# Sums of gathered tiles tied to an even beat, and the first group's ranks with 128 columns of weights, in a graph layer on one core

## The chip, the core and the metric

The kernel runs on one core of a Trainium2 chip. The metric is the device time of the program in microseconds (us), without the profiler: the median of the runs. The engines are TensorE (PE in the profile, PEld for its weight loads), VectorE (DVE), ScalarE (ACT), GpSimd (POOL) and SyncE (SP), each with an instruction queue of its own that is worked off in order. SP and POOL issue most DMAs here.

## The reference

A graph layer with 6,250 nodes of 128 features and 100,000 edges, sorted by target node. Each edge carries a message, the source's row times one of two weight matrices (by the type of the edge). Messages are summed at the target, a third matrix's product is added, then ReLU, the residual and a normalisation over the features.

```python
Xs = X[src]
m_data = Xs @ W_data.T + b_data
m_ctrl = Xs @ W_control.T + b_control
msg = jnp.where((edge_types == 0)[:, None], m_data, m_ctrl)
agg = jax.ops.segment_sum(msg, dst, num_segments=X.shape[0])
out = jax.nn.relu(agg + (X @ W_self.T + b_self))
return _layernorm(X + out, axis=-1)
```

## The kernel before

**Build.** The nodes are 49 blocks of 128 rows. For each block the kernel multiplies the rows with the two message matrices (`y`, L465 and L467) and splits the f32 result into three bf16 parts that add up to it (`yh`, `y1`, `ym`, `y2`, `yl`: copies on ACT or DVE, matmuls with `minus` at L483 and L496). The three parts stay in SBUF as `m3` (98 tables of 128 rows by 3 × 128) and are also stored to DRAM as `table`, part by part, in seven pairs of stores on SP (L509). Parts hold 4, 8, 8, 8, 8, 8 and 5 blocks; they are numbered from 0.

**Two ways to sum.** Target blocks 0 to 34 are in seven groups of five and are summed from SBUF ("windowed" blocks). Blocks 35 to 48 are summed from DRAM ("gathered" blocks): for each, 18 tiles of 128 edges are fetched by POOL with an indirect DMA from `table` (`msg`, L877), and TensorE adds each one into the block's sum with a one-hot matrix as weights (`gm`, tile `agg_g`, L231). There are 14 × 18 = 252 such tiles. `msg` has MB = 5 buffers: a fetch can start when the fifth sum before it is done. DVE makes the one-hot matrices for six tiles at once (`gh`, tile `hot_g`).

**Windowed blocks.** For each group the edges that fall into its window are sorted into buckets by source table. `fields` and `hot` prepare one-hot matrices (`hot_st`), and a rank of each edge within its bucket is found in 18 steps: TensorE adds `tri` times the one-hot matrix into an accumulator (`tri`, tile `acc`), DVE reads the ranks out (`rank`, tile `slot`, L584), TensorE adds the remainder (`rest`). Both matmuls go through the helper `by_columns` (L231), which makes four matmuls with 32 columns of weights each of one with 128. Once six steps are ranked, DVE makes `two` and TensorE writes the edges' numbers into their slots (`v`, tile `small`, L621, ten matmuls for a step). After the 18th, ACT copies the slots (`vs`), SP stores them (`packed`, L639) and loads them back as a broadcast to all partitions (`rows`, L739), one load for a block. DVE turns that into one-hot weights (`sel`, L746); TensorE gathers from `m3` with them (`g`, tile `g_ps`, L775), ACT copies the result out (`e`, tile `gs`, L790), and TensorE sums it into the target rows (`s`, tile `agg`, L231). A block takes 25 tiles of `g` and as many of `s`. Then come `o` (the product with the third matrix), `whole`, `sum`, and normalisation and store, a group at a time (`root`, `scale`, `apply`, `out`).

**Order.** Nothing in the order of the instructions is left to the chip. Each kind of step is a generator that names the step, what it costs on which engine, and what it needs. `Order.run` plays them through on a clock of its own and always takes the step that can start first; among those that can start within 0.1 us of each other the one with the earliest due time (`due`). `BUILT`, `BLOCK` and `PACE` set the due times. So a changed cost or due time moves instructions of all engines, whether or not the chip's times agree with the planner's. In it a step `msg` keeps POOL busy for `PACE` and is there 3.0 us after its start.

Of the kernel before, what the change touches and what calls it, by code (L numbers as in the profile page):

```python
# [19 lines left out]
P = 128  # L20
# [7 lines left out]
KT = 18  # L28
# [24 lines left out]
CH = 6  # L53
KC = 6
# [4 lines left out]
class Order:  # L59
# [10 lines left out]
    CLOSE = 0.1  # L70

    def __init__(self):
        self.free = dict.fromkeys("TVAGS", 0.0)
        self.end = {}

    def run(self, streams, due):
# [24 lines left out]
def step(name, costs, *needs, lag=0.0):  # L101
    return as_tuple(name), costs, [as_tuple(n) for n in needs], lag
# [111 lines left out]
def sums_over_windows(ctx, tc, x, xt, edges, w, bias, table, packed, total,  # L214
                      add_parts, finish, load_rows, norm):
    nc = tc.nc
    V, A, G, T = nc.vector, nc.scalar, nc.gpsimd, nc.tensor
# [7 lines left out]
    order = Order()  # L225
    YB = 4

    def by_columns(out, lhsT, rhs, **flags):

        for c in range(0, P, 32):  # L230
            T.matmul(out[c : c + 32], lhsT[:, c : c + 32], rhs, **flags)  # L231


    r0 = const.tile([EC, RJ], I32, name="r0")
# [49 lines left out]
    for j in range(RJ):  # L284
# [7 lines left out]
        out=er.rearrange("p k c -> p (k c)"), out_offset=None,  # L292
# [90 lines left out]

    LEAD, BUILT = 6.0, 76
    BLOCK = 13.1
    PACE = 1.68
    AHEAD, FIRST = 26.0, 20

    def due(kind, *i):
# [35 lines left out]
        if kind in ("rows", "sel", "d", "g", "e", "s"):  # L425
            of = {"rows": 1, "sel": 1, "d": 2}.get(kind, NS)
            lead = {"rows": -9, "sel": -3, "d": -1, "g": 0, "e": 1, "s": 2}[kind]
            return BUILT + BLOCK * (i[0] + (i[1] / of if len(i) > 1 else 0)) + lead
        if kind in ("gh", "gm", "msg"):
            k = i[1] * CH if kind == "gh" else i[1]  # L430
            return BUILT + PACE * (i[0] * KT + k) + {"msg": 0, "gh": 2, "gm": 5}[kind]
        n = GROUPS[i[0]]
        end = BUILT + BLOCK * STARTS[i[0]] - (AHEAD if i[0] else FIRST)
        span = BLOCK * n if i[0] else 34.0
# [136 lines left out]
    def ranks():  # L571
        for grp, n in enumerate(GROUPS):
            free = [("rank", grp - 1, KT - 1)] if grp else []
            for k in range(KT):
                yield step(("tri", grp, k), {"T": 0.21}, ("hot", grp, k // KC), *free)
                if k == 0:
                    acc = ps_a.tile([P, 512], F32, name="acc")
                    flat = acc[:, : n * NT]
                    by_q = flat.rearrange("p (s q) -> p q s", q=n)
                hot = hots[grp, k // KC][:, k % KC].rearrange("p s q -> p (s q)")  # L580
                by_columns(flat, tri, hot, start=k == 0, stop=False, skip_group_check=True)
                free = []
                yield step(("rank", grp, k), {"V": 0.13 + 0.103 * n}, ("tri", grp, k))
                V.tensor_reduce(slots[grp][:, k, :], by_q, axis=AX.X, op=ALU.max)  # L584
                if k == KT - 1:
                    break
                yield step(("rest", grp, k), {"T": 0.21}, ("rank", grp, k))
                by_columns(flat, rest, hot, start=False, stop=k == KT - 2, skip_group_check=True)

    def fill_a():  # L590
        for grp, n in enumerate(GROUPS):
# [16 lines left out]
    def fill_b():  # L608
        for grp, n in enumerate(GROUPS):
            free = [("listed", grp - 1)] if grp else ["first"]  # L610
            for k in range(KT):
                yield step(("v", grp, k), {"T": 0.07 * n}, ("two", grp, k // KC), *free)
                if k == 0:
                    vts[grp] = ps_a.tile([P, 512], F32, name="small")
                vt = vts[grp][:, : (n + 1) // 2 * NT].rearrange("p (j s) -> p j s", s=NT)
                two = two_s[grp, k // KC]
                hot = hots[grp, k // KC]
                for q in range(n):
                    for i in range(2):
                        c0 = (q % 2 * 2 + i) * R  # L620
                        T.matmul(vt[c0 : c0 + R, q // 2, :], two[:, k % KC, i, :, q],  # L621
                                 hot[:, k % KC, :, q], start=k == 0 and q < 2,
                                 stop=k == KT - 1, skip_group_check=True)
                free = []
# [247 lines left out]
    def gather_rows():  # L872
        for i, (j, k) in enumerate(gathered):
            free = [("gm", *gathered[i - MB])] if i >= MB else [*stored, "idx"]
            yield step(("msg", j, k), {"G": PACE}, *free, lag=3.0 - PACE)
            msgs[j, k] = late.tile([P, D3], BF16, name="msg", bufs=MB)
            G.indirect_dma_start(  # L877
                out=msgs[j, k], out_offset=None, in_=table[:, :],
                in_offset=bass.IndirectOffsetOnAxis(ap=idx[:, j, k : k + 1], axis=0),
            )  # L880

    def gathered_hots():
        chunks = [(j, c) for j in range(NG) for c in range(KT // CH)]
# [9 lines left out]
    def gathered_sums():  # L893
        for j, k in gathered:
            free = [("agg", NPB + j)] if k == 0 else [("o", NPB + j)] if k == KT - 1 else []
            yield step(("gm", j, k), {"T": 0.165}, ("msg", j, k), ("gh", j, k // CH), *free)
            if k == 0:
                aggs[NPB + j] = ps_a.tile([P, D3], F32, name="agg_g")
            by_columns(aggs[NPB + j], g_hots[j, k // CH][:, :, k % CH], msgs.pop((j, k)),
# [28 lines left out]
    def close_build():  # L928
# [9 lines left out]
        normalise([(lambda g=g: (hs_[g], mvs[g]), STARTS[g] + q0, q0, n) for g, q0, n in PIECES], "p"), add_up(), gather(), evict(), to_hots(), bucket_hots(),  # L938
        multiply(), take(0, "yh", "y"), leave(0, "y1", "yh"),
        take(1, "ym", "y1"), last_part(), constants(), store(), close_build(), add_counts(),  # L940
        finish_gathered(), gathered_sums(), gathered_hots(), gather_rows(), gathered_fields(),
        normalise([(lambda i=i: kept[i], NPB + i * GQ, 0, min(GQ, NG - i * GQ))
                   for i in range(-(-NG // GQ))], "g"),
        load_own("p", list(range(NPB)), XS),
# [128 lines left out]
```

## Time and profile before

| what | value |
|---|---|
| median of 3 runs without the profiler | 627.68 us (622.87 to 630.16) |
| the profiled execution's own time | 542.67 us |
| its span, first to last instruction | 540.9 us |
| mean granted TensorE clock in it | 0.984 |
| busy: PE, DVE, ACT, POOL | 507.3, 432.4, 415.9, 297.4 us |
| matmuls | 11,204 |

Durations below are from the one profiled execution. Busy time is a union of recorded intervals on an engine, and matmuls overlap in it. "Idle before" names what ended an engine's idle time. The chain of work follows the last instruction back, at each step to what released it. A granted clock of 0.5 in a window means that TensorE ran at half speed there.

### The profile page before, as it was taken

The numbers are of one execution on the slowest core, as the hardware profiler recorded it, in microseconds if no ns is written. First come the engines' busy times: TensorE is split into PE (matmuls) and PEld (weight loads), VectorE is DVE, ScalarE is ACT, GpSimd is POOL, SyncE is SP. The second block draws the span as 40 slices with busy tenths as digits, with TensorE's granted clock in tenths as the row PEclk, the third lists the DMA queues.
The fourth block names the chain that finished last, engine by engine and source line by source line (L and its number), as shares of the span: only waits on it lengthen the run. The fifth ranks groups of instructions, "written<-read, shape, count | busy, mean of one in ns | idle before, by whom it ended". The sixth has DMA issues, their size and how long they took to land.

```text
span 540.9 us, 26355 instructions
## 1 busy us (share of the span) xinstructions
PE 507.3 (94%) x11204; PEld 442.9 (82%) x11204; DVE 432.4 (80%) x967; ACT 415.9 (77%) x1003; POOL 297.4 (55%) x267
## 2 busy tenths in 40 slices
PE   5799977999999999999999999999999999999993
PEld 3546547799887998988989899999998999889882
DVE  5587889578987789978799878999789667668784
ACT  6654356577869788798888888877979879889793
POOL 1000002777687676776567676775757756677500
PEclk9999998799999999999999999999999999999998
DMA  3566875542555425554354542544445454555301
GB/s 94 145 179 191 260 239 193 153 131 79 184 159 161 138 77 179 157 169 134 99 194 139 164 139 81 183 139 160 142 134 162 133 156 135 180 166 164 115 17 35
DMA packets 60932, 79.19 MB, mean 146 GB/s; under 512 B 15760, under 2 KB 51371, under 8 KB 60807
## 3 DMA queue, kind: packets, MB, share of 16 engines
q1 hardware_dynamic: 47253, 49.14, 27.8%
q0 software_dynamic: 12400, 25.08, 16.9%
q10 hardware_dynamic: 1154, 3.21, 1.9%
q8 instruction: 89, 1.46, 1.1%
q14 instruction: 36, 0.29, 0.2%
HBM read 64.35 MB, written 13.05 MB: 143 GB/s over the span
## 4 chain that ended last, share of the span: by engine, by line
PE 73%; DMA 9%; ACT 5%; DVE 5%; issue 3%; SPq 3%; POOL 1%; ACTq 0%; DVEq 0%; POOLq 0%
PE agg L231 25%; PE g_ps L775 23%; PE acc L231 8%; PE agg_g L231 7%; PE small L621 6%; DMA msg<-table,idx 5%; ACT gs L790 2%; DMA rows<-packed 2%; PE y L465 2%; SPq L807 1%; POOL msg L877 1%; ACT h_p L189 1%; SPq L158 1%; DVE slot L584 1%; DVE hot_st L567 1%
## 5 line engine op out<-in xcount | busy, mean ns | idle before, releaser
L790 ACT CAST gs<-g_ps 128x384 bf16<-128x384 f32 x807 | 333.7, 498 | 72.4 <-PE g_ps L775 53.5
L877 POOL DMA_INDIRECT msg<-table,idx x252 | 288.5, 1145 | 115.4 <-PE g_ps L775 46.4
L775 PE MATMUL g_ps<-m,rows 128*32 128x384 bf16 x3430 | 322.4, 332 | 0.9 <-ACT gs L790 0.7
L231 PE MATMUL agg<-gs,hot_d 128*32 128x384 bf16 x3360 | 301.4, 331 | 3.3 <-ACT gs L790 3.3
L231 PEld LDWEIGHTS <-hot_d 128*32 128x32 bf16 x3500 | 195.8, 137 | 13.1 <-issue 7.1
L775 PEld LDWEIGHTS <-rows 128*32 128x32 bf16 x3430 | 189.8, 137 | 18.5 <-issue 12.7
L231 PE MATMUL agg_g<-msg,hot_g 128*32 128x384 bf16 x1008 | 109.1, 332 | 6.2 <-DMA msg<-table,idx 5.8
L584 DVE TENSOR_REDUCE slot<-acc 128x5 bf16<-128x490 f32 x126 | 83.6, 663 | 28.9 <-PE acc L231 17.7
L760 DVE TENSOR_TENSOR hot_d<-count,to 128x1664 bf16<-128x1664 bf16 x70 | 74.4, 1065 | 6.6 <-PE agg L231 6.0
L621 PE MATMUL small<-hot_st,two 128*32 128x98 bf16 x1260 | 70.2, 290 | 0.0
L231 PE MATMUL acc<-hot_st,tri 128*32 128x490 bf16 x504 | 61.8, 376 | 2.1 <-DVE hot_st L567 2.1
L231 PEld LDWEIGHTS <-hot_g 128*32 128x32 bf16 x1008 | 53.5, 123 | 10.6 <-issue 7.8
L231 PE MATMUL acc<-hot_st,rest 128*32 128x490 bf16 x476 | 56.8, 378 | 4.5 <-DVE slot L584 4.0
L621 PEld LDWEIGHTS <-two 128*32 128x32 bf16 x1260 | 58.3, 118 | 2.3 <-DVE two L605 0.6
L715 POOL DMA_INDIRECT mixed<-table,row_i x7 | 6.5, 933 | 92.9 <-DVE hot_g L889 82.3
L476 ACT CAST m<-y 128x512 bf16<-128x512 f32 (+1 forms) x50 | 28.1, 577 | 30.9 <-PE y L483 23.1
L567 DVE TENSOR_TENSOR hot_st<-count,st_b 128x2940 bf16<-128x2940 bf16 x21 | 41.8, 1996 | 7.6 <-PE small L621 5.3
L746 DVE TENSOR_SCALAR rows<-rows,pid 128x3136 bf16<-128x3136 bf16 x35 | 37.0, 1057 | 5.5 <-DMA rows<-packed 5.2
L153 DVE TENSOR_REDUCE whole<-agg 128x128 f32<-128x384 f32 x35 | 19.4, 553 | 17.6 <-PE agg L231 12.8
L465 PE MATMUL y<-w_sb,xt 128*128 128x256 f32 x98 | 33.2, 426 | 0.0
L231 PEld LDWEIGHTS <-rest 128*32 128x32 bf16 x476 | 22.1, 98 | 12.8 <-issue 11.8
L231 PEld LDWEIGHTS <-tri 128*32 128x32 bf16 x504 | 22.4, 99 | 3.3 <-issue 3.1
(144 smaller groups left out, 438.0 us busy)
## 6 DMA issues: line engine op xcount, KB each, us to landing
rows<-packed SPq DMA_DIRECT2D x35, 784.0 KB
table<-m SPq DMA_DIRECT2D x10, 768.0 KB
msg<-table,idx POOLq DMA_INDIRECT x252
xt<-in_xt ACTq DMA_DIRECT2D x5, 512.0 KB
xt_p<-in_xt SPq DMA_DIRECT2D x35, 64.0 KB
xs_p<-in_x SPq DMA_DIRECT2D x35, 64.0 KB
out<-h_p SPq DMA_DIRECT2D x6, 320.0 KB
table<-m SPq DMA_DIRECT2D x2, 480.0 KB
```

The lines of the kernel that those rows point to most:

```text
L153: nc.vector.tensor_reduce(whole, agg.rearrange("p (i c) -> p c i", i=3), axis=AX.X, op=ALU.add)
L231: T.matmul(out[c : c + 32], lhsT[:, c : c + 32], rhs, **flags)
L465: T.matmul(y[:, j, :], xts[g][:, b + j - at_part[g], :], w_sb[:, : 2 * D], start=j == 0, stop=False, skip_group_check=True)
L476: A.copy(part_of(b, n, i), ys[b][:, :n, :].rearrange("p b (t c) -> p t b c", t=2))
L567: V.tensor_tensor(hot, counted[n][:, None, 1 : NT + 1, :].to_broadcast([P, KC, NT, n]), fields[grp][2][:, c * KC : c * KC + KC, None, :].t ...
L584: V.tensor_reduce(slots[grp][:, k, :], by_q, axis=AX.X, op=ALU.max)
L621: T.matmul(vt[c0 : c0 + R, q // 2, :], two[:, k % KC, i, :, q], hot[:, k % KC, :, q], start=k == 0 and q < 2, stop=k == KT - 1, skip_group ...
L746: V.tensor_scalar(rows[b], rows[b], pid1, None, op0=ALU.is_equal)
L760: V.tensor_tensor(hot, counted[DC][:, :, :n], places[grp][:, q, None, c * DC : c * DC + n].to_broadcast([P, P, n]), op=ALU.is_equal)
L775: T.matmul(g_ps[t * R : (t + 1) * R, :D3], rows[b][:, :, s], m3[:, s, :], start=True, stop=True)
L790: (A.copy if e == "A" else V.tensor_copy)(gs[at], g_tiles.pop((b, g))[at, :D3])
L877: G.indirect_dma_start(out=msgs[j, k], out_offset=None, in_=table[:, :], in_offset=bass.IndirectOffsetOnAxis(ap=idx[:, j, k : k + 1], axis=0),
```

## The change

Three things change. The ranks of group 0 are made with weights of 128 columns (`width`), one matmul where there were four; the other groups keep 32. The slots of group 0 are written in chunks: all 60 matmuls of six steps in one planner's step. And the sums of gathered tiles get a beat: a fictitious engine "C" in the planner, on which a step `beat` of `PACE` runs for every gathered tile from 4 us after the table's stores are planned to be in; `gm` waits for its beat and gets an earlier due time. `msg` now costs POOL 1.25 in the planner and its data is there 3.0 us after that; `PACE` is 1.75 instead of 1.68. The beat puts no instruction on the chip: it only moves the planned place of `gm`.

```diff
@@ class Order
-        self.free = dict.fromkeys("TVAGS", 0.0)
+        self.free = dict.fromkeys("TVAGSC", 0.0)
...
-    def by_columns(out, lhsT, rhs, **flags):
-
-        for c in range(0, P, 32):
-            T.matmul(out[c : c + 32], lhsT[:, c : c + 32], rhs, **flags)
+    def by_columns(out, lhsT, rhs, width=32, **flags):
+
+        for c in range(0, P, width):
+            T.matmul(out[c : c + width], lhsT[:, c : c + width], rhs, **flags)
...
-    PACE = 1.68
+    PACE = 1.75
...
+        if kind in ("beat", "beating"):
+            return 0.0
         if kind in ("gh", "gm", "msg"):
             k = i[1] * CH if kind == "gh" else i[1]
-            return BUILT + PACE * (i[0] * KT + k) + {"msg": 0, "gh": 2, "gm": 5}[kind]
+            return BUILT + PACE * (i[0] * KT + k) + {"msg": 0, "gh": 2, "gm": 0}[kind]
...
@@ def ranks():
+            width = 32 if grp else P
...
-                by_columns(flat, tri, hot, start=k == 0, stop=False, skip_group_check=True)
+                by_columns(flat, tri, hot, width, start=k == 0, stop=False, skip_group_check=True)
...
-                by_columns(flat, rest, hot, start=False, stop=k == KT - 2, skip_group_check=True)
+                by_columns(flat, rest, hot, width, start=False, stop=k == KT - 2, skip_group_check=True)
...
@@ def fill_b():
-                yield step(("v", grp, k), {"T": 0.07 * n}, ("two", grp, k // KC), *free)
+                if grp:
+                    yield step(("v", grp, k), {"T": 0.07 * n}, ("two", grp, k // KC), *free)
+                elif k % KC == 0:
+                    yield step(("v", grp, k + KC - 1), {"T": 0.07 * n * KC}, ("two", grp, k // KC), *free)
...
@@ def gather_rows():
-            yield step(("msg", j, k), {"G": PACE}, *free, lag=3.0 - PACE)
+            yield step(("msg", j, k), {"G": 1.25}, *free, lag=3.0)
...
+    def beats():
+
+        yield step("beating", {"C": 4.0}, *stored, "idx")
+        for i, (j, k) in enumerate(gathered):
+            yield step(("beat", j, k), {"C": PACE}, "beating")
...
@@ def gathered_sums():
-            yield step(("gm", j, k), {"T": 0.165}, ("msg", j, k), ("gh", j, k // CH), *free)
+            yield step(("gm", j, k), {"T": 0.165}, ("msg", j, k), ("beat", j, k), ("gh", j, k // CH), *free)
```

The first place where the order moves is SP's queue, at the end of the build. Before, the slots of group 0 stand behind the loads of block 3, and the stores of table part 5 come after the first three `rows`:

```order
L807 DMA xt_p_958<-in_xt 128x128
L158 DMA xs_p_960<-in_x 128x128
L639 DMA packed_61<-vs0_151 32x3x98
L639 DMA packed_61<-vs0_151 32x2x98
L739 DMA rows_1124<-packed_61 128x3136
L739 DMA rows_1126<-packed_61 128x3136
L739 DMA rows_1141<-packed_61 128x3136
L509 DMA table_60<-m3_157 128x8x384 x2
L509 DMA table_60<-m3_157 128x5x384 x2
```

Now the pair of part 5 (eight blocks) stands ahead of `packed`:

```order
L813 DMA xt_p_844<-in_xt 128x128
L158 DMA xs_p_846<-in_x 128x128
L511 DMA table_60<-m3_157 128x8x384 x2
L645 DMA packed_61<-vs0_151 32x3x98
L645 DMA packed_61<-vs0_151 32x2x98
L745 DMA rows_1030<-packed_61 128x3136
L745 DMA rows_1034<-packed_61 128x3136
L745 DMA rows_1036<-packed_61 128x3136
L511 DMA table_60<-m3_157 128x5x384 x2
```

The loads ahead of it are the same as before in number, so `packed` has two more stores in front of it, of 768 KB each.

The second place is TensorE's queue in the build, between the seventh and the eighth step of group 0's ranks. Before, four weight loads and matmuls with 32 columns for `rest` and as many for `tri` (the three repeats of each are left out) stand between matmuls with 128 columns:

```order
L467 MATMUL y<-bias_104,ones_b 128x256
L231 LDWEIGHTS rest
L231 MATMUL acc<-hot_st,rest 32x490
...
L231 LDWEIGHTS tri
L231 MATMUL acc<-hot_st,tri 32x490
...
L621 LDWEIGHTS two
L621 MATMUL small<-hot_st,two 32x98
```

Now it is one each; the 60 matmuls of `v` follow, with 32 columns as before:

```order
L469 MATMUL y<-bias_104,ones_b 128x256
L231 LDWEIGHTS rest
L231 MATMUL acc<-hot_st,rest 128x490
L231 LDWEIGHTS tri
L231 MATMUL acc<-hot_st,tri 128x490
L627 LDWEIGHTS two
L627 MATMUL small<-hot_st,two 32x98
```

The number of changes between matmuls of 128 and of 32 columns falls from 46 to 15, counted from the first rank matmul to the first of `g_ps`.

The third place is TensorE's queue at the seventh and eighth gathered tile of block 35. Before, their sums follow each other directly (buffer numbers are kept; of four equal pairs of rows one is shown):

```order
L621 MATMUL small_1267<-hot_st_865,two_1794 32x98
L231 LDWEIGHTS hot_g_1933
L231 MATMUL agg_g_1591<-msg_1785,hot_g_1933 32x384
...
L231 MATMUL agg_g_1591<-msg_1845,hot_g_1933 32x384
L231 LDWEIGHTS tri_143
L231 MATMUL acc_950<-hot_st_1066,tri_143 32x490
```

Now six tiles of windowed blocks, a step of `v` and a `rest` stand between them (most are left out):

```order
L231 MATMUL agg_g_1421<-msg_1490,hot_g_1664 32x384
L231 LDWEIGHTS hot_d_1348
L231 MATMUL agg_1685<-gs_1718,hot_d_1348 32x384
...
L781 LDWEIGHTS rows_1034
L781 MATMUL g_ps_1795<-m3_157,rows_1034 32x384
...
L231 LDWEIGHTS rest_144
L231 MATMUL acc_867<-hot_st_966,rest_144 32x490
L231 LDWEIGHTS hot_g_1664
L231 MATMUL agg_g_1421<-msg_1545,hot_g_1664 32x384
```

Counted over the whole queue in tiles of `g` and `s`: ahead of the first gathered sum stand 42 before and 32 now; behind the last one 86 before and 23 now. The smallest number over five spacings is 16 before and 19 now.

More of the change, by code (lines that the diff above doesn't have):

```diff
@@ L940, in sums_over_windows @@
         take(1, "ym", "y1"), last_part(), constants(), store(), close_build(), add_counts(),
-        finish_gathered(), gathered_sums(), gathered_hots(), gather_rows(), gathered_fields(),
+        finish_gathered(), gathered_sums(), gathered_hots(), gather_rows(), gathered_fields(), beats(),
         normalise([(lambda i=i: kept[i], NPB + i * GQ, 0, min(GQ, NG - i * GQ))
```

## The prediction

> **What bounds the kernel now.** I read the page's busy shares first, then the windows of equal length, then the chain of work and the waits of TensorE.
>
> ```profile
> PE 507.3 (94%) x11204; PEld 442.9 (82%) x11204; DVE 432.4 (80%) x967; ACT 415.9 (77%) x1003; POOL 297.4 (55%) x267
> PE 73%; DMA 9%; ACT 5%; DVE 5%; issue 3%; SPq 3%; POOL 1%; ACTq 0%; DVEq 0%; POOLq 0%
> ```
>
> TensorE is busy for 94% of the span and carries 73% of the chain that ended last. A busy record is longer than the time a matmul takes from its successor:
>
> ```profile
> 240.37 0.40 PE L231 MATMUL agg<-gs,hot_d 128*32 128x384 bf16 x4
> 240.53 0.40 PE L775 MATMUL g_ps<-m,rows 128*32 128x384 bf16 x4
> ```
>
> A tile (four matmuls beside each other, one for each 32 columns of weights) is recorded as 0.40 us, but the next one starts 0.16 us later. So 0.16 us is the price of a tile, and a wait shorter than about 0.24 us leaves no idle time in a record. Where TensorE does idle in the long stage is in the waits from 95 to 520 us (engine, what it waited for: total, times, longest):
>
> ```profile
> PE agg_g L231 <- DMA msg<-table,idx: 5.8, 7, 3.5
> PE agg L231 <- ACT gs L790: 3.3, 6, 1.0
> PE acc L231 <- DVE slot L584: 0.8, 3, 0.3
> ```
>
> The largest item is the one that the change is about: a sum over a gathered tile (`gm`) waiting for its message. Since hidden stalls count too, I went through the starts in the timeline:
>
> ```profile
> 104.23 0.39 PE L231 MATMUL agg<-gs,hot_d 128*32 128x384 bf16 x4
> 104.89 0.38 PE L231 MATMUL agg_g<-msg,hot_g 128*32 128x384 bf16 x4 [0.27 <-DMA msg<-table,idx]
> 514.45 0.39 PE L231 MATMUL agg_g<-msg,hot_g 128*32 128x384 bf16 x4
> ```
>
> From 104.23 to 104.89 there are 0.66 us where a tile needs 0.16, so this sum lost 0.5 us though the record shows 0.27. Counted so, 22 of the sums after 100 us come over 0.12 us late, the first at 104.89 and the last at 514.45, together **9.4 us**. That is the most that an even spacing can give in this stage.
>
> The front is another matter. There the SP queue and the transfers set the pace:
>
> ```profile
> 61.94 0.43 SPq L158
> 62.48 0.38 SPq L509
> 62.90 0.58 SPq L509
> 63.52 1.63 SPq L807
> 65.20 1.23 SPq L158
> 66.48 1.20 SPq L807
> 68.74 0.43 SPq L158
> 69.27 3.25 DMA packed<-vs
> 72.54 5.28 DMA rows<-packed
> 77.84 1.04 DVE rows L746
> ```
>
> These are pieces of the chain of work. SP issues without a pause up to 69.27: two table stores (L509), then loads, of which the first three take 1.63, 1.23 and 1.20 us instead of 0.43. Then come the packed slots of group 0, the broadcast `rows` and the first select. The first gather out of `rows` follows at 79.92, and the messages only later:
>
> ```profile
> 79.92 1.71 PE L775 MATMUL g_ps<-m,rows 128*32 128x384 bf16 x20
> 91.54 1.60 POOL L877 DMA_INDIRECT msg<-table,idx  x1 [0.30 <-ACT gs L790]
> 94.91 0.53 PE L231 MATMUL agg_g<-msg,hot_g 128*32 128x384 bf16 x4 [3.50 <-DMA msg<-table,idx]
> ```
>
> TensorE stood for 3.5 us at the first gathered sum, and its clock paid for it (per window of 4 us: busy of five engines, granted clock, DMA share, GB/s):
>
> ```profile
> 64.00:68.00 4.00, 3.94 (x76) 2.73 (x78) 2.79 (x5) 0.99 (x2) 0.00 (x0) 1.00 1.03 315
> 80.00:84.00 4.00, 4.00 (x97) 3.27 (x93) 3.96 (x6) 2.01 (x5) 0.00 (x0) 0.57 1.05 373
> 84.00:88.00 4.00, 4.00 (x106) 4.00 (x102) 3.90 (x9) 3.21 (x8) 0.00 (x0) 1.00 1.04 346
> 96.00:100.00 4.00, 4.00 (x56) 2.63 (x52) 0.00 (x0) 1.75 (x4) 3.09 (x4) 0.50 0.45 114
> ```
>
> **The change part by part.** *Ranks with 128 columns.* The price of changing between 128 and 32 columns of weights stands here:
>
> ```profile
> 48.33 0.27 PE L467 MATMUL y<-bias,ones_b 128*128 128x256 bf16 x1
> 48.53 0.39 PE L231 MATMUL acc<-hot_st,rest 128*32 128x490 bf16 x4
> 48.75 0.38 PE L231 MATMUL acc<-hot_st,tri 128*32 128x490 bf16 x4
> 49.06 0.39 PE L483 MATMUL y<-m,minus 128*128 128x256 bf16 x2
> ```
>
> `rest` to `tri` takes 0.22 us for 490 columns, so the 256 of L467 should take 0.11; they take 0.20. `tri` takes 0.31 where 0.21 would do. Each change costs 0.10 us. From the first rank matmul to the first gather the old order has 46 changes and the new one 15 (the chunks of `v` remove some, too). The work itself stays: one pass of 490 columns for four beside each other. So TensorE gains 31 × 0.10 = 3.1 us in the build. I count this as **0**: it lies under the SP queue, which had no gap from 55.7 to 69.2. Without that cover it would be worth 3.1 us.
>
> *Slots in chunks, and what moves on SP.* The chunk of `v` now stands behind three more `y`, so in the planner's account `packed` becomes later, and the pair of stores of table part 5 goes ahead of it. Those two DMAs cost 1.05 us of issue (62.48 to 63.52), and what follows a pair is slow: two issues at 1.63 and 1.23 instead of packed's 1.04 and 0.42, 1.4 us more. `packed` then lands at 69.27 + 3.25 + 2.45, about 75.0. The lower end is 1.05 alone; the upper end is that `packed` lands only when the pair's 1,536 KB are through: at 315 GB/s that is 5.0 us from 69.27, then the 1.8 us that packed took after its second issue, 76.1, or 3.6 late. I take **+3.0**, nearer the upper end, since three slow issues behind the pair show its data still moving.
>
> The Trainium skill speaks against the change here: its page "DMA: Bandwidth & Descriptors", section "Queues, rings and completion order", says that a DMA engine takes the descriptors of one ring in their order. By that rule the start slips 3.6 us; if the small stores could pass the large ones it would slip 1.05. The trace agrees so far as the slow issues go; no row shows a `packed` behind a pair.
>
> *The first gathered sum.* The messages wait for all table stores. With part 5 stored earlier, three `rows` of 784 KB and the last pair of 480 KB each are left, 3.3 MB; at 346 to 373 GB/s that takes 9.2 us from about 76.1, to 85.3 instead of 88. So messages begin some 2.6 us sooner and the first sum can run at about 92.3 instead of 94.91. Ahead of it stand 32 tiles instead of 42 in the new order. Before, 42 tiles took from 79.92 to 91.41 (0.27 us each); from 82.9 on, 32 take 8.7 us, to 91.6. So the 3.5 us wait shrinks to 0.7. Arriving 2.6 us earlier with 10 tiles less done, worth 1.6 us at 0.16 or 2.7 at 0.27, nets **−0.5** (0 to −1.0), with the late start inside it. If the clock then stays up, half of the 5.4 us at half speed is saved, 2.7; bounds 0 and −2.7. I take **−2.2**, because shorter waits, such as that at 104.89, lie in windows of nearly full clock.
>
> *The beat.* The old planner let POOL's queue set the pace and put `gm` where a free place was, so two sums follow each other directly and the next comes late. Five buffers mean that a gather starts when the fifth sum before it is done.
>
> ```profile
> L231 PE MATMUL agg_g<-msg,hot_g x1008: 323/326/528, 94.9 to 516.1; 128*32 128x384 bf16 x168
> 98.45 6.40 DMA msg<-table,idx
> ```
>
> (first: count, shortest/median/longest ns, first and last start; then a piece of the chain.) 252 sums from 94.9 to 516.1 are 1.68 us apart, so five are 8.4 us on average, and the longest landing among the chain's large pieces is 6.40 from issue, 6.7 with the 0.30 that POOL waits. Evenly spaced, no message would be late. In the order, the smallest number of tiles over five spacings goes from 16 to 19, and spacings of 0 or 1 tile become rare, not absent. The gain lies between 0 and −9.4; near its upper end by these rows, but ACT and DVE slots behind the sums shift with it, so I take **−6.5**.
>
> *The tail.* After the last gathered sum 86 tiles were left, now 23. Before, they ran from 516.26 to 532.1, 15.8 us for 14.0 of tiles, so up to 1.5 us can go. But the last four gathered blocks are now normalised at the very end:
>
> ```profile
> 516.53 0.55 DVE L153 TENSOR_REDUCE whole<-agg_g 128x128 f32<-128x384 f32 x1
> 525.62 0.39 SPq L196 DMA_DIRECT2D out<-h_g  x1
> 531.98 0.41 PE agg L231 x4
> 535.47 0.49 ACT h_p L189
> ```
>
> That took 9.1 us from its first sum to its store, among other work. The last windowed block needs 4.0 from its last tile to its apply. With 23 tiles (about 4 us) between, the gathered tail could end 1 to 1.5 us later. I take **−0.5**.
>
> **Sum.** −0.5 − 2.2 − 6.5 − 0.5 = −9.7 us, from 542.67 to 533.0. The median without the profiler is 627.68, 85 us more; nothing in the trace shows what they are. I carry the difference over as it is: **618.0**. In proportion it would be 616.5.
>
> **Rivals.** *The waits only move: no change that can be told (1% of 627.68, 6.3 us, is about what a measurement tells).* For it: ACT's evictions already hold TensorE for 3.3 recorded us, and the order on DVE and ACT shifts everywhere. Against it: messages are the larger item. With 2 to 3 us from the front and as much from the rest, −5, or 623; with none, 628. Chance 0.33. The same holds if the beat evens out the plan but not the chip.
>
> *Slower by the SP queue.* SP takes its DMAs in order. If the pair of part 5 is not ready when SP comes to it, `packed` stands behind a wait. In the old order the last copy for that pair ended at 75.05:
>
> ```profile
> 74.46 0.59 ACT L501 CAST m<-y 128x512 bf16<-128x512 f32 x1
> ```
>
> Issued then, `packed` lands at 75.05 + 1.05 + 2.7 + 1.8 = 80.6 and gathers start 8.1 us late; a TensorE that is full afterwards doesn't win that back, and if the sums behind gain nothing either, the time is 627.68 + 8 = 636. It decides from the point where the slip of the first gather exceeds what the vanished waits give, 9.7 + 3.0 in my sum. Against it: the new order brings that part's multiplications ahead of the chunk, so its copy should end several us before 69. Chance 0.12.
>
> *More than forecast.* If the 85 us hold longer message waits than the profiled execution, an even spacing gives more, up to twice my sum: 608. Nothing speaks for it but that gap. Chance 0.05.
>
> The forecast itself, 612 to 621, gets 0.50. That makes 0.55 for faster by over 1%, 0.33 within, 0.12 slower. The range 608 to 630 takes in the forecast, the first rival and the larger gain.
>
> **What would show it.** Right: message waits of TensorE under 2 us in total after 95 us; the first gather at 82 to 84 us; the first gathered sum at 92 to 93 with a granted clock near 1 behind it; changes of mode gone from the build without an earlier start; last gathered sum some 4 us ahead of the last tile. Wrong: a start before 80 (SP was not the bound), `gs` waits grown by as much as message waits fell, or the end set by the stores of `h_g`.

## The result and the profile after

The changed kernel takes **607.04 us** (median of 4 runs, 606.19 to 607.68), the kernel before 627.16 beside it (622.87 to 630.16): ratio 0.9683, 95% interval 0.9624 to 0.9742. The forecast was 618.0 with 608 at the lower end. The direction was right, the gain twice as large, and the time lies below the range.

The experiments below ran on four chips: the kernel before takes about 545 us on one of them and 625 to 634 us on the three others, at the same mean granted clock (0.98 to 0.99). Its profile quoted in the prediction (542.67) lies at the first level, while all timed runs of both kernels and the profile after (606.19, span 604.1) lie at the second; on which chips those ran is not on record. Below, the first is called the fast chip and the others slower chips; only one chip was fast, in one set of runs, so that it is the chip and not something else of those runs is not shown. For a comparison on equal ground I took a profile of the kernel before on one of the slower chips (626.12, span 624.3) and use that as the "before" here.

The pages, busy time of the engines, after and then before on a slower chip:

```profile
PE 535.1 (89%) x11099; PEld 440.7 (73%) x11099; DVE 435.0 (72%) x971; ACT 418.7 (69%) x999; POOL 293.5 (49%) x267
```

```profile
PE 549.0 (88%) x11204; PEld 443.2 (71%) x11204; DVE 433.7 (69%) x967; ACT 420.8 (67%) x1003; POOL 290.1 (46%) x267
```

VectorE, ScalarE and GpSimd are busy as long as in the profile of 542.67 (432.4, 415.9, 297.4). The 83 us that the span is longer are not slower instructions of theirs. They are starts of TensorE that come late, as the windows of 100 us show (busy time of five engines with the number of instructions, granted clock, DMA share, GB/s): after, then before on a slower chip, then before on the fast chip.

```profile
200.00:300.00 100.00, 93.21 (x2108) 78.52 (x2104) 77.13 (x180) 74.26 (x187) 61.61 (x55) 1.00 0.44 131
```

```profile
200.00:300.00 100.00, 88.55 (x1905) 72.79 (x1900) 68.70 (x150) 69.02 (x170) 58.29 (x51) 0.98 0.40 119
```

```profile
200.00:300.00 100.00, 97.80 (x2381) 88.46 (x2376) 87.22 (x209) 82.96 (x209) 69.20 (x62) 1.00 0.50 148
```

In the same 100 us TensorE starts 2,381 matmuls on the fast chip, 1,905 on a slower one, 2,108 there after the change. The change wins back part of a loss that the profile I predicted from did not contain.

TensorE's waits in the long stage (engine, waited for: total, times, longest), after and then before on a slower chip:

```profile
PE agg L231 <- ACT gs L796: 15.4, 32, 1.6
PE agg L231 <- issue: 6.9, 15, 1.3
PE g_ps L781 <- issue: 6.0, 13, 1.3
PE g_ps L781 <- ACT gs L796: 3.7, 9, 1.1
```

```profile
PE agg L231 <- ACT gs L790: 11.9, 27, 1.6
PE g_ps L775 <- issue: 10.8, 20, 1.8
PE g_ps L775 <- ACT gs L790: 9.9, 19, 1.4
PE agg L231 <- issue: 8.5, 24, 0.8
```

Messages are not among these: 0.3 us in this stage before, nothing after. Late are the gathers out of `rows` and their sums, 40 to 47% of it with no wait that the profile knows ("issue"). For each start of TensorE between the first and the last gathered sum I took the time since the start before it, less the price of the matmuls between (0.16 us a tile and so on, as in the prediction), and added this up. These start gaps are 31.9 us for before on the fast chip, 112.5 on a slower one, 91.2 after. In the build (20.4 against 22.0 on the fast chip) and behind the last gathered sum (1.5 against 1.6) the chips don't differ. The loss begins and ends with the gathered tiles.

What a single loss looks like: TensorE and ScalarE in before on a slower chip, then both in a kernel without gathers (below).

```profile
119.31 0.39 PE L775 MATMUL g_ps<-m,rows 128*32 128x384 bf16 x4
120.59 0.48 ACT L790 CAST gs<-g_ps 128x384 bf16<-128x384 f32 x1 [1.32 <-PE g_ps L775]
121.12 0.39 PE L775 MATMUL g_ps<-m,rows 128*32 128x384 bf16 x4 [1.42 <-ACT gs L790]
```

```profile
116.56 0.39 PE L775 MATMUL g_ps<-m,rows 128*32 128x384 bf16 x4
117.05 0.48 ACT L790 CAST gs<-g_ps 128x384 bf16<-128x384 f32 x1 [0.26 <-PE g_ps L775]
```

In the second, ScalarE reads a tile 0.49 us after the tile's first matmul started (0.43 after its last). In the first it takes 1.28 us: ScalarE is idle and waits, TensorE issues nothing, and then the loop goes on. The trace has the times of the semaphores, the signals by which one engine tells another that a step is done. Here TensorE's signal comes 0.90 us after the last matmul of the tile started; 0.35 us is usual in the profiles of the fast chip.

To count such cases without guessing which matmul an engine waited for, I looked for signals of TensorE that come over 0.9 us after the start of the last matmul that could have sent them, between the first and the last gathered sum. There are none in before on the fast chip, 73 in before on a slower one (of 1,203 signals), 63 after. VectorE's and ScalarE's signals, where they have a record (on the slower chip some 27% have none), come within 0.1 us of the end of their instruction. Where a sum of TensorE had to wait, it starts 0.05 us after the end of its eviction in most cases on both chips, also in most of those called "issue", which are then waits for a signal without a record. So it is mostly TensorE's finished work that is reported late. Whether the matmul itself ends late or only its signal is not shown, since the profile works out the ends of matmuls and does not record them.

The gathers' own time shows in these cases: half of the 73 signals come 1.37 to 1.73 us after POOL began a gather, where the gathers are about 2.0 us apart.

### The profile page after: what moved, and what is told of

Read it like the earlier page. It is cut to its first block, busy times and chain, and to the rows that moved or that the text cites. A ratio compares the mean times of both kernels' runs of the same rounds, so it can differ in the third digit from the quotient of the medians.

```text
span 604.1 us, 26148 instructions
## 1 busy us (share of the span) xinstructions
PE 535.1 (89%) x11099; PEld 440.7 (73%) x11099; DVE 435.0 (72%) x971; ACT 418.7 (69%) x999; POOL 293.5 (49%) x267
## 4 chain that ended last, share of the span: by engine, by line
PE 75%; ACT 7%; SPq 5%; DVE 5%; issue 4%; DMA 3%; ACTq 0%; another core or an unknown queue 0%; DVEq 0%
PE agg L231 27%; PE g_ps L781 26%; PE agg_g L231 7%; PE acc L231 7%; PE small L627 6%; ACT gs L796 4%; SPq L369 2%; SPq L373 2%; DVE slot L587 1%; ACT h_p L189 1%; DMA packed<-vs 1%; DMA rows<-packed 1%; PE y L467 1%; DVE hot_st L569 1%; ACT h_g L189 1%
## 5 line engine op out<-in xcount | busy, mean ns | idle before, releaser
L883 POOL DMA_INDIRECT msg<-table,idx x252 | 283.3, 1124 | 200.6 <-PE g_ps L781 120.2
L781 PE MATMUL g_ps<-m,rows 128*32 128x384 bf16 x3430 | 330.0, 333 | 15.1 <-issue 6.0
L231 PE MATMUL agg<-gs,hot_d 128*32 128x384 bf16 x3360 | 307.9, 336 | 23.0 <-ACT gs L796 15.4
L231 PEld LDWEIGHTS <-hot_d 128*32 128x32 bf16 x3500 | 201.4, 137 | 59.3 <-issue 49.9
L781 PEld LDWEIGHTS <-rows 128*32 128x32 bf16 x3430 | 186.5, 138 | 40.6 <-issue 29.6
L231 PE MATMUL acc<-hot_st,tri 128*32 128x490 bf16 (+1 forms) x450 | 59.8, 375 | 2.3 <-DVE hot_st L569 2.3
L231 PE MATMUL acc<-hot_st,rest 128*32 128x490 bf16 (+1 forms) x425 | 53.2, 374 | 6.5 <-DVE slot L587 5.4
L467 PE MATMUL y<-w_sb,xt 128*128 128x256 f32 x98 | 30.5, 397 | 0.0
L796 DVE CAST gs<-g_ps 128x384 bf16<-128x384 f32 x36 | 19.4, 554 | 13.9 <-PE g_ps L781 11.3
L231 PEld LDWEIGHTS <-rest 128*32 128x32 bf16 (+1 forms) x425 | 20.3, 99 | 10.9 <-issue 8.7
```

The costliest lines, as they stand in the source:

```text
L231: T.matmul(out[c : c + width], lhsT[:, c : c + width], rhs, **flags)
L467: T.matmul(y[:, j, :], xts[g][:, b + j - at_part[g], :], w_sb[:, : 2 * D], start=j == 0, stop=False, skip_group_check=True)
L781: T.matmul(g_ps[t * R : (t + 1) * R, :D3], rows[b][:, :, s], m3[:, s, :], start=True, stop=True)
L796: (A.copy if e == "A" else V.tensor_copy)(gs[at], g_tiles.pop((b, g))[at, :D3])
L883: G.indirect_dma_start(out=msgs[j, k], out_offset=None, in_=table[:, :], in_offset=bass.IndirectOffsetOnAxis(ap=idx[:, j, k : k + 1], axis=0),
```

## Experiments

**Parts of the change, on the fast chip** (before: 544.6 us). First the kernel before once more, with a profile.

> The kernel before, unchanged, to see an execution near its median of 627 us rather than the 542.67 us of the one profiled so far. Message theory: TensorE's waits for gathered messages, 5.8 us in the short execution, are 20 us or more in an ordinary one, and the other waits are as in the changed kernel's profile. Fetch theory: messages stay below 10 us, and the missing 85 us are stalls that no wait explains (issue) and waits for evictions, as in the changed kernel's profile, where TensorE's weight loads stood 69 us before issue against 29.7 in the short execution.

545.35 us. TensorE waited 7.5 us for messages, where the profile I predicted from has 5.8. The chip is the fast one, so this run had none of the missing 85 us and tested neither theory. The next three expectations are given for a kernel before of 627 us and can be held against the ratio only.

*The beat alone* (the lines on `width` and the chunks of `v` undone):

```diff
-            width = 32 if grp else P
+            width = 32
-                if grp:
-                    yield step(("v", grp, k), {"T": 0.07 * n}, ("two", grp, k // KC), *free)
-                elif k % KC == 0:
-                    yield step(("v", grp, k + KC - 1), {"T": 0.07 * n * KC}, ("two", grp, k // KC), *free)
+                yield step(("v", grp, k), {"T": 0.07 * n}, ("two", grp, k // KC), *free)
```

> The changed kernel with group 0's ranks back at 32 columns and its slots step by step: the beat alone. If the beat carries the gain (message theory), 606 to 611 us, ratio to before 0.965 to 0.975. If the front carries it (a build theory: fewer changes of width, table part 5 stored earlier), 622 to 628. If both share it, 612 to 620.

538.67 us, ratio 0.9897 (0.9865 to 0.9928). That is less gain than the first theory has (0.965 to 0.975) and agrees with none of the three clearly. Of the waits for messages one is left, that at the first gathered sum:

```profile
PE agg_g L231 <- DMA msg<-table,idx: 4.2, 1, 4.2
```

*Ranks and chunks alone* (the other half of the diff, on the kernel before):

> The kernel before with group 0's ranks at 128 columns and its slots in chunks, no beat, the old pace. Message theory: 622 to 630 us, no difference that can be told. Build theory: 607 to 615. The prediction's own account: the SP queue hides the gain in the build, so within 3 us of before.

546.64 us, ratio 1.002 (0.9991 to 1.0049): no effect that can be told.

*The change without the beat's wait*:

```diff
-            yield step(("gm", j, k), {"T": 0.165}, ("msg", j, k), ("beat", j, k), ("gh", j, k // CH), *free)
+            yield step(("gm", j, k), {"T": 0.165}, ("msg", j, k), ("gh", j, k // CH), *free)
```

> The changed kernel with its sums no longer tied to the beat; the pace of 1.75, POOL's cost of 1.25 and the earlier due time stay. If the even spacing matters, the sums crowd or lag again: message waits come back, 615 to 630 us. If only the due time and POOL's cost matter, 605 to 610.

546.41 us, ratio 1.0046 (1.0014 to 1.0078), and the waits for messages are there again. The beat carries the gain; cheaper `msg` costs and earlier due times without it give none. The whole change was not run on the fast chip.

```profile
PE agg_g L231 <- DMA msg<-table,idx: 10.6, 9, 2.0
```

**On a slower chip** (before: 626.95 us), the change again, before with eight message buffers (`MB, XB = 8, 2`), before with a profile, and the change with the stores of table part 5 held behind the first three `rows`.

> The changed kernel, unchanged, beside the kernel before on one chip. Where before takes some 544 us, my own sum (9.7 us less) gives 535, ratio 0.982; the beat alone gave 0.990 there. Where before takes some 627 us, 607 again, ratio 0.968. If the ratio on the 544 us level is 0.968 as well, 527, the level has nothing to do with the size of the gain.

608.33 us, ratio 0.9719 (0.9674 to 0.9765), as expected for this level.

> The kernel before with eight message buffers instead of five (MB = 8), nearly the same order: a fetch can start eight sums ahead. Message theory: the waits for messages go without any beat, 535 to 540 us where before takes 544, 600 to 612 where it takes 627. If it is the order on the other engines that the beat improves, no change within 0.5%.

657.06 us, ratio **1.0467** (1.0417 to 1.0517). More buffers let messages start earlier, and the kernel became 30 us slower, which neither expectation had. Waits for messages were no limit there. TensorE starts fewer matmuls than before's 1,905 in the same window:

```profile
200.00:300.00 100.00, 85.09 (x1855) 71.13 (x1851) 63.81 (x136) 64.59 (x158) 54.27 (x48) 0.97 0.38 110
```

The granted clock fell as well, to a mean of 0.952 against 0.983 in before. As an estimate from the two spans, up to 21 of the 30 us are lost clock; it is low in windows in which TensorE starts few matmuls (0.83 from 240 to 260 us, with 229).

> The kernel before once more, for a profile on the chip of this call. On the 544 us level as before. On the 627 us level: message theory, waits for messages of 20 us or more counted by the starts of the sums; fetch theory, stalls before issue and late evictions of 70 to 90 us, messages some 10 to 15.

626.12 us; its profile is the "before" above. Messages are waited for 3.9 us in all, so the message theory is out; the start gaps are 81 us above those of the fast chip, as the fetch theory had it, though it had more message waits.

```diff
-                yield step(("table", g, t), {"S": 0.5}, ("yl", last), lag=6.0)
+                yield step(("table", g, t), {"S": 0.5}, ("yl", last), *([("rows", 2)] if g == 5 else []), lag=6.0)
```

> The changed kernel with the stores of table part 5 held back in the planner until the first three broadcasts, so that the packed slots come ahead of them again. My prediction's account: the first gather starts 1.5 to 3 us sooner than in the changed kernel, near 80 us, but messages later; total within 0.5% of the changed kernel, no more than 3 us faster. If the SP order costs what the slower rival said, 3 us or more faster.

604.36 us, ratio 0.9639 (0.9599 to 0.968): 4.0 us less than the change beside it, which is what the slower rival said (3 us or more) and not my own account. TensorE's first gather moves from 81.76 to 79.62 (after and then this kernel):

```profile
81.76 0.87 PE L781 MATMUL g_ps<-m,rows 128*32 128x384 bf16 x8 [4.38 <-DVE rows L752]
```

```profile
79.62 2.16 PE L781 MATMUL g_ps<-m,rows 128*32 128x384 bf16 x24
```

**The parts again, on another slower chip** (before: 633.88 us), same kernels as above.

> The kernel after, unchanged, beside its own parts. The kernel before has been seen at about 544 us and at about 627 us, in different calls, at equal granted clock. Theory A (the beat gives one fixed amount, the vanished message waits and the shorter tail, some 6 us, and the slower level adds its own gain in the TensorE stalls): beside a kernel before of 544 us the ratio is 0.985 to 0.992 (536 to 540), beside one of 627 us 0.968 to 0.976 (607 to 612). Theory B (the gain is a share of the time at either level): 0.97 at both, 528 us beside 544.

612.63 us, ratio 0.9678 (0.963 to 0.9725), which does not tell the two theories apart.

> The beat without the 128-column ranks and the chunks of slots. Theory A: all of the gain is the beat's; beside a kernel before of 627 us the time is within 4 us of the kernel after beside it (607 to 613), beside 544 us it is 537 to 540. Theory C (the level of 627 us needs the other table order too): 617 to 623 beside 627 us.

603.72 us, ratio **0.9513** (0.947 to 0.9555): the beat alone takes off 30 us and is the fastest version that computes the layer. Both theories missed that: it is 9 us below the whole change. In its profile the first gathered sum comes at 96.35 us, in that of the whole change at 98.77, and in the whole change some 16 fewer tiles of `g` and `s` are done ahead of it. As an estimate that makes 2.4 us and, at 0.16 us a tile, another 2.6; where the rest of the 9 us goes is not shown.

> The kernel before with the 128-column ranks and the chunks of slots of group 0 alone, no beat. Theory A: within 0.5% of the kernel before at either level (624 to 630 beside 627 us, 543 to 548 beside 544 us). Theory C: 610 to 618 beside 627 us.

634.34 us, ratio 1.0002 (0.9977 to 1.0028).

> The kernel after, but with gathered sums that don't wait for their beat in the planned order; all other numbers of the change stay. Theory A: the spacing carries the gain, so the time is that of the kernel before within 0.6% (544 to 548, or 623 to 631). Rival: at 627 us the gain comes from the moved due time of gathered sums and the shorter tail, not from their spacing: 607 to 614.

641.56 us, ratio 1.0105 (1.0061 to 1.0149). The time is 0.4% above what theory A allowed, and no gain is left without the spacing: here too all hangs on it, and the beat's gain is five times that on the fast chip. A fixed gain from vanished message waits does not explain it.

**The gathers themselves**, on a third slower chip (before: 625.46 us). All kernels of this part but the one with four buffers sum rows that are not the true messages, so they do not compute the layer and show times only. Without gathers after the first five:

```diff
+            if i >= MB:
+                msgs[j, k] = first_msgs[i % MB]
+                continue
```

> The kernel before, in the same planned order, but only the first five messages are gathered; all later sums use these five tiles again (247 gathers left out). In the runs of 627 us TensorE hesitated (a read of a finished matmul came late, its next matmul too) only between the first and the last gathered sum: 112.5 us of start gaps beyond the price of the matmuls against 31.9 in a run of 545 us, and as much in build and tail. Theory G (the running gathers hold TensorE up): beside a kernel before of 627 us it falls to 530 to 545, and handoffs from TensorE to ScalarE come at the 0.43 us of the fast runs. Theory H (the hesitation belongs to the chip, not to the gathers): only the message waits go, 615 to 624. Beside 544 us both give 530 to 538.

541.36 us, ratio **0.8654** (0.8623 to 0.8686). This is the time of the fast chip. Of TensorE's signals 3 are late by the count above, where before has 73, and the start gaps fall to 29.1 us.

```diff
-            G.indirect_dma_start(
-                out=msgs[j, k], out_offset=None, in_=table[:, :],
-                in_offset=bass.IndirectOffsetOnAxis(ap=idx[:, j, k : k + 1], axis=0),
-            )
+            G.dma_start(out=msgs[j, k], in_=table[i % NT * P : (i % NT + 1) * P, :])
```

> The kernel before with each gather replaced by a plain load of 128 rows in a row from the same table into the same buffer, on the same queue (the rows are not those of the indices). Theory G1 (what hurts is the indirect form: POOL's making of the addresses): 535 to 550 beside a kernel before of 627 us. Theory G2 (what hurts is the data that comes in, 98 KB a tile): 610 to 630. Theory H: as G2.

539.65 us, ratio **0.8624** (0.8582 to 0.8666). As many tiles come in over the same queue, TensorE has no late signal, and it starts 2,333 matmuls in the window where it started 1,905 in before:

```profile
200.00:300.00 100.00, 96.58 (x2333) 89.27 (x2328) 85.93 (x199) 83.92 (x211) 35.64 (x62) 1.00 0.50 155
```

The loads' row on the page, and that of the gathers in before (line, engine, operation, count; busy, mean ns; idle before):

```profile
L877 POOL DMA_DIRECT2D msg<-table x252 | 144.1, 574 | 251.1 <-PE agg_g L231 144.4
```

```profile
L877 POOL DMA_INDIRECT msg<-table,idx x252 | 281.2, 1116 | 204.5 <-PE g_ps L775 88.9
```

An indirect one keeps POOL busy for 1.12 us, a plain one for 0.57. On POOL's queue of DMAs both kernels move the same packets (the plain loads first):

```profile
q0 software_dynamic: 12400, 25.08, 16.5%
```

```profile
q0 software_dynamic: 12400, 25.08, 15.0%
```

The Trainium skill says in "DMA: Bandwidth & Descriptors", section "SWDGE vs HWDGE vs iDMA", that GpSimd builds the descriptors of its DMAs in software, for direct and indirect ones. The plain loads go that way too and cost nothing here, so that this alone is not it.

> The beat alone (ranks and slots as before), with only the first five messages gathered. If the even spacing helps only by what it does to gathers, this is within 3 us of the kernel before without gathers beside it. If the order of the other work gained too (the shorter tail), it is 4 to 12 us below that.

538.06 us, ratio 0.8593 (0.8557 to 0.8628). Without gathers the beat gains 3.3 us, where it gained 30 with them: at the border between the two expectations, so that most of its gain on a slower chip goes through the gathers, and the order of the other work gives a small part at most.

> The beat alone with four message buffers in place of five. Eight buffers in the kernel before made it 4.7% slower. If gathers that run beside each other hold TensorE up, four buffers are faster than five: beside a kernel before of 627 us 590 to 600 where five gave a ratio of 0.951 (596). If the lost spacing of landing times costs more (a message then has four spacings, 7.0 us, to land in, and the longest took 6.7), 600 to 615. Beside 544 us: 540 to 548.

608.06 us, ratio 0.9723 (0.9683 to 0.9762), inside the second range and not the further gain over five buffers that fewer gathers in flight were to bring: four leave as many gathers close together (17 against 15, below). The reason given with that range did not show, since no wait for a message is left in the profile. The beat with five ran on another slower chip, so the 2% between the ratios are only a hint that four are worse.

Then, on the same chip (before: 627.11 us), indirect gathers of rows in a row:

```diff
-        V.tensor_add(idx, far, win_g[:, :, :, 0])
+        true = work.tile(shape, I32, name="true_g", bufs=1)
+        V.tensor_add(true, far, win_g[:, :, :, 0])
+        G.iota(idx, pattern=[[P, NG], [4 * P, KT]], base=0, channel_multiplier=1)
```

> The kernel before, whose gathers stay indirect, but with indices that name 128 rows in a row (made by POOL once, the true ones are computed and not used). Plain loads of rows in a row took the kernel from 625 to 540 us. Theory G1a (the indirect instruction itself, POOL's work on addresses and the list it writes, holds TensorE up): 615 to 632 beside a kernel before of 627 us. Theory G1b (the scattered reads of the table do): 538 to 555. Beside 544 us both give 541 to 547.

627.16 us, ratio 1.0006 (0.9969 to 1.0042). Scattered reads are not the cause; the indirect form of the DMA is.

```diff
+            if i % 2:
+                G.dma_start(out=msgs[j, k], in_=table[i % NT * P : (i % NT + 1) * P, :])
+                continue
```

> The kernel before with every second gather (126 of 252) replaced by a plain load of 128 rows in a row. Theory L (each indirect gather costs TensorE the same, 84 us / 252 = 0.33 us): 578 to 588 beside a kernel before of 627 us. Theory O (gathers that follow each other closely cost more than single ones, so that spacing alone helps): the pairs are gone, and it is 550 to 572.

559.51 us, ratio **0.8953** (0.8889 to 0.9017). Without any indirect gather the kernel would take 541 to 543 by the two ratios above. So half of the gathers cost 17 to 19 us, all of them 84 to 86: the cost is far from proportional, as theory O has it. That alone leaves another reading, that a full TensorE hides half of the delays. The traces decide for closeness.

They show what follows a gather, as the mean number of matmuls that TensorE starts in the 2 us from a gather's start (gathers from 110 to 520 us):

| profile | gather (or load) under 1.3 us after the one before | others |
|---|---|---|
| before, fast chip | 47 (85 gathers) | 48 |
| before, slower chip | 21 (21) | 40 |
| change, three profiles | 24; 24; 22 (12; 11; 10) | 42; 42; 42 |
| beat alone, slower chip | 18 (10) | 42 |
| before, indices in a row, slower chip | 19 (22) | 40 |
| before, all plain, slower chip | 47 (70) | 47 |

So on a slower chip a gather right behind another costs TensorE about half of these 2 us, any other one a tenth to a seventh, and a plain load nothing that shows. The numbers of such gathers in the whole run, and TensorE's start gaps between the first and the last gathered sum:

| kernel, slower chips | gathers under 1.3 us apart | start gaps, us |
|---|---|---|
| before; with ranks and chunks; indices in a row | 30; 27; 32 | 112.5; 116.7; 114.9 |
| change without the beat's wait | 34 | 124.9 |
| change, three profiles | 15; 15; 14 | 91.2; 89.0; 91.0 |
| beat alone; with four buffers | 15; 17 | 91.3; 92.3 |
| before, eight buffers | 52 | 144.3 |
| before, half of the loads plain | 0 of 126 | 45.3 |
| before, no gathers; all plain | – | 29.1; 27.7 |

As an estimate from four of these rows (28 without gathers, 112.5 at 30, 91 at 15, 144.3 at 52): 1.4 us for each close pair and 0.17 us for every gather. That would give 49 us for the half, where 45.3 were measured. The row with eight buffers holds lost clock too, so the shares are rough. On the fast chip the kernel before has 91 to 93 close pairs and 31.9 us of gaps: there they cost nothing.

## Why the prediction was wrong

**The step that failed** is the last of the sum: "nothing in the trace shows what they are. I carry the difference over as it is." The 85 us between the profiled execution and the median were no constant. On a slower chip 84 to 86 us go when the indirect gathers do, and the change takes off a part of just that: 30 us by the beat, of which 9 are lost again to the rest of the change. The rival that named the 85 us ("if the 85 us hold longer message waits") had the right place, with a chance of 0.05, but the wrong mechanism. In before on a slower chip TensorE waited for messages (total, times, longest):

```profile
PE agg_g L231 <- DMA msg<-table,idx: 3.9, 2, 3.6
```

Of these 3.6 us lie at the first gathered sum. That the rival's 608 comes near the measured 607.04 is luck: it is twice the sum, while the measured gain is 30 us less 9. With 85 of 628 us unexplained, that rival deserved far more.

**The beat, −6.5.** On the fast chip the beat alone gave 5.9 us, and the message waits vanished as described. But the upper end of 9.4 us was not what it was called: in before with only the first five messages gathered, 6.4 us of late starts are still counted ahead of gathered sums, and the beat still gains 3.3 us there. Counting by starts finds the loss, not its cause. On a slower chip the term is 30 us for the beat alone.

**Start of the gathers, +3.0.** In the chain of work of after:

```profile
69.13 6.82 DMA packed<-vs
75.97 4.23 DMA rows<-packed
80.23 1.05 DVE rows L752
81.32 1.50 PE g_ps L781 x12
```

`packed` lands at 75.95 where 75.0 was expected, 3.4 us later than in the profile before (72.52). That is near the upper bound of 3.6 and far from 1.05, so the pair ahead of it holds it up. The Trainium skill's rule in "DMA: Bandwidth & Descriptors", section "Queues, rings and completion order", that a ring's descriptors are taken in order, goes with the upper bound, and the trace agrees with it. The broadcast then takes 4.23 us instead of 5.28, so the first gather slips less: it starts at 81.32 to 81.94 in three profiles against 79.0 to 79.9 in three of before, on average 2.1 us late where 3.0 were taken. What this costs at the end was sized too small: undoing it gave 4.0 us.

**Ranks with 128 columns, 0.** Right beside the kernel before: 1.002 and 1.0002. The first gather did not come sooner by fewer changes between 128 and 32 columns; `packed` behind the pair set it. Beside the beat, ranks and chunks cost 9 us, which the sum had not.

**The first gathered sum and the clock.** The timeline of TensorE after, with the first and the last gathered sum and the last tile, and a window of 4 us:

```profile
93.55 0.38 PE L231 MATMUL agg_g<-msg,hot_g 128*32 128x384 bf16 x4 [1.21 <-DMA msg<-table,idx]
589.38 0.39 PE L231 MATMUL agg_g<-msg,hot_g 128*32 128x384 bf16 x4
594.27 0.39 PE L231 MATMUL agg<-mixed,hot_d 128*32 128x384 bf16 x4
```

```profile
96.00:100.00 4.00, 2.11 (x23) 0.98 (x21) 1.20 (x2) 1.27 (x3) 2.22 (x4) 1.00 0.29 77
```

The first sum runs at 93.55 instead of 92.3, with a wait of 1.21 us; in the other two profiles it comes at 95.08 and 98.77, against 93.97 in before on a slower chip. The messages begin at 90.61, not 2.6 us but 0.9 us sooner than in the profile before (91.54), and 0.3 us sooner beside before on the same slower chip (90.71 against 91.03). The clock stays at 1.00 from 96 to 100 us, as hoped, but TensorE starts only 23 matmuls there. In another profile of the change it starts 56 at a clock of 1.00, against 35 at 0.70 in before on the same chip. So whether the 2.2 us were collected is not shown.

**The tail, −0.5.** From the last gathered sum to the last tile it is 4.9 us (4 expected), from there to the end 9.8 instead of 8.8 us, near the 1 to 1.5 us that were put down for the finish of the gathered blocks. That this finish is the cause is not shown: the beat alone has the short tail too and ends 9.0 us after its last tile.

**The signs named in advance** were met for the messages (in the profile after none is waited for after 95 us, under 2 us expected). The sign against it, `gs` waits that grow, was met beside the profile of the fast chip (4.0 to 19.1) and not on equal ground (21.8 to 19.1). Signs read across two levels would have misled.

## What to carry to other kernels

Before a profile is used to size a change, its time has to agree with the timed runs; an unexplained part of 85 in 628 us is a term of the sum, and a change that touches what may cause it needs a range that shows this. A wait list tells what an engine waited for, not what slowed it: the loss here stood under "issue" and under evictions, and only leaving out the suspected instructions showed the cause. Where indirect gathers run beside a full TensorE, as here, try to spread them evenly and look for plain loads; eight buffers in place of five made it worse, and four gave no sign of being better.

## What the runs showed of the hardware

- Indirect DMAs from POOL held up TensorE on one chip by 84 to 86 us for 252 gathers, shown by leaving them out (541.36 of 625.46 us). Plain loads of as many bytes on the same queue cost nothing (539.65). On two other chips of the same level the traces show the same loss behind close gathers (18 to 24 matmuls started in 2 us, against 40 to 42 behind others); on the fast chip they show none (47 against 48).
- TensorE's signals then come late: 73 of 1,203 over 0.9 us after the last matmul that could have sent them, none in before on the fast chip.
- The order of the rows doesn't matter (ratio 1.0006), closeness does (half of the gathers, a fifth of the cost).
- What in the instruction does it, and why one chip is free of it, stays open. The price for each close pair is an estimate that fits these rows; the runs rule out a cost in proportion to the number of gathers.
